# First column of the scan's addend made on ScalarE: three quarters of the scans begin from zero instead of from the carried state

## The chip, the cores and the metric

The program runs on one core of a Trainium2 chip. The core has five engines that each work through a queue of their own, in order: TensorE (PE, matmuls, with its weight loads shown apart as PEld), VectorE (DVE), ScalarE (ACT), GpSimd (POOL) and SyncE (SP, which here only issues transfers). They meet through semaphores. The metric is the device time of one execution in microseconds (us).

## The reference

Two layers follow each other, each as `x = x + layer(groupnorm(x))`, on an input of 4 x 512 x 64 x 64 in fp32. The second is a linear attention over 4096 positions. The first is what matters here: a layer norm over 512 channels, the channels cut into four chunks of 128, and for each chunk a Mamba block with 256 inner channels and 16 states per channel. Its heart is a recurrence over the 4096 positions of an image:

```python
dt = jax.nn.softplus(jnp.einsum('blr,er->ble', dt, dt_proj_w) + dt_proj_b)
A = -jnp.exp(A_log)

def step(h, inp):
    dt_t, B_t, C_t, x_t = inp
    dA = jnp.exp(dt_t[:, :, None] * A)
    h = dA * h + (dt_t * x_t)[:, :, None] * B_t[:, None, :]
    y = jnp.einsum('bds,bs->bd', h, C_t)
    return (h, y)
```

So for each of 4 images x 4 chunks x 256 channels x 16 states there is one scan `h[t] = dA[t] * h[t-1] + bx[t]` along 4096 positions, and the result is multiplied by C and summed over the 16 states.

## The kernel before

**Tiles.** The positions of an image are cut into 8 tiles of T = 512. A step is one triple (image b, tile t, chunk c), with c innermost: 4 x 8 x 4 = 128 steps, in `steps`. Within a step the 256 channels x 16 states are laid out as 32 groups of 128 partitions (32 channels x 4 states each), so a step has 32 scans of 128x512, and the program has 4096. Two scans make a slot; a step has SLOTS = 16 slots, numbered 0 to 15. Scan number k belongs to slot k // 2 of the whole program; `place` turns that number into the step n, the channel half e, the state group q and the half jj of the pair of slots.

**One scan.** Its operands come from three engines. `decay(k)` (L825) lets ACT write dA = exp(A * dt) into one of LEAD = 3 PSUM banks. `drive(g)` (L833) lets POOL make bx for both scans of slot g in one 128x1024 product, into one of 3 buffers. `slot` issues the scans on DVE (L851), with `tensor_tensor_scan`, whose initial value is the literal 0.0 in the first tile of an image (t == 0) and else a column of `st`, an SBUF tensor of 128x1 columns that holds the last value of the same scan one tile earlier. After every second slot POOL copies the four new last values into `st` (L862) and multiplies the last quarter of h by C (L863); DVE multiplies the first three quarters by C (L871, `product`), and PE folds the states (`fold_states`).

**Order.** The whole main loop is written out by hand in issue order, so each engine's queue is fixed when the program is built. In slot g: POOL's `drive(g + 2)`; then, for each of the two scans, the scan k on DVE and after it the exp of scan k + LEAD on ACT, which may start when scan k has given back its PSUM bank. Between the two scans (after the second in slot 10) of every even slot comes `product` of the slots before. After the two scans `after()` issues the step's other work by slot number: in slot 3 a softplus between two table loads on ACT (`time_steps`, L728, with table loads L1343 and L1345), in slot 10 the silu between two table loads (L1220, L1221, L1365), and in other slots copies of y, of projections, group and layer norms and the pieces of attention, many of which are ACT instructions. AWAY = (3, 10) names the two slots with the table loads.

**What one slot waits for.** A scan needs its dA (ACT), its bx (POOL) and, when it is the first of four, that PE is done with the h buffer. An exp needs a free PSUM bank, so the scan three before it. A drive needs the bx buffer of the slot three before it.

Of the kernel before, what the change touches and what calls it, by code (L numbers as in the profile page):

```python
# [10 lines left out]
AF = mybir.ActivationFunctionType  # L11
ALU = mybir.AluOpType
# [12 lines left out]
def kernel(  # L25
# [24 lines left out]
    nc = tc.nc  # L50
# [16 lines left out]
    LEAD = 3  # L67
# [338 lines left out]
    def bc(v, n):  # L406
        return v.unsqueeze(1).to_broadcast([P, n, v.shape[-1]])
# [346 lines left out]
    def mixers(f, nm):  # L754

        pd = work_bank(f"pd_{nm}", 0)
        for e in range(NH):
            mm(pd, w_xp[:, e, :], f["xz"][:, 0, e, :], start=(e == 0), stop=(e == NH - 1))  # L760
        yield
        f["both"] = wk.tile([P, 2, NH, T], F32, tag="dt", name=f"dt_{nm}", bufs=1)
        dtr = f["dtr"] = f["both"][0 : 2 * LANE, 1, NH - 1, :]
        nc.scalar.copy(dtr, pd[0 : 2 * LANE, :])
        b_rows = f["b_rows"] = dram.tile([NST, T], F32, tag="b_rows", name=f"b_rows_{nm}", bufs=3)
        c_rows = f["c_rows"] = dram.tile(
            [NST, T - CUT], F32, tag="c_rows", name=f"c_rows_{nm}", bufs=3
        )

        def rows_out():  # L770
            nc.sync.dma_start(b_rows, dtr[RANK : RANK + NST, :])
            nc.sync.dma_start(c_rows, dtr[LANE : LANE + NST, CUT:])

        later(1, rows_out)
        parts = f["parts"] = wk.tile([P, CUT], BF16, tag="parts", name=f"parts_{nm}", bufs=3)
        nc.scalar.copy(parts, pd[:, :CUT])
        for i in (2, 3):
            yield
            mm(pd[:, :CUT], minus, parts, start=False, stop=True, skip_group_check=True)
            yield  # L780
            nc.scalar.copy(parts[i * LANE :, :], pd[i * LANE :, :CUT])  # L781
# [4 lines left out]
    SLOTS = NH * NQ * JJ  # L786
    AWAY = (3, 10)

    def place(g):

        n, r = divmod(g, SLOTS)
        e, r = divmod(r, NQ * JJ)
        return n, e, *divmod(r, JJ)

    b_all, c_all, c_sb, dAs, bxs, hs, ys = {}, {}, {}, {}, {}, {}, {}
# [8 lines left out]
    def b_row(g):  # L804
        n, e, q, _ = place(g)
        b_all[g // JJ] = wk.tile([P, T], F32, tag="b_all", name=f"b_all_{g}", bufs=3)
        for_states(b_all[g // JJ], fs[n]["b_rows"], q)

    def c_tail(g):
        n, e, q, _ = place(g)  # L810
        c_sb[g // JJ] = wk.tile([P, T - CUT], F32, tag="c_sb", name=f"c_sb_{g}", bufs=2)
        for_states(c_sb[g // JJ], fs[n]["c_rows"], q)
# [7 lines left out]
    def decay(k):  # L820

        n, e, q, jj = place(k // 2)
        j = jj * 2 + k % 2
        dAs[k] = ps_d.tile([P, T], F32, tag="dA", name=f"dA_{k}")
        nc.scalar.activation(  # L825
            dAs[k], fs[n]["d_all", e][:, 0, j, :], AF.Exp, scale=a_t[:, e, j, q : q + 1]
        )

    def drive(g):

        n, e, q, jj = place(g)
        bxs[g] = wk.tile([P, 2, T], F32, tag="bx", name=f"bx_{g}", bufs=3)
        nc.gpsimd.tensor_tensor(  # L833
            bxs[g], fs[n]["d_all", e][:, 1, jj * 2 : jj * 2 + 2, :], bc(b_all[g // JJ], 2), ALU.mult
        )

    def slot(g, last, after):
        n, e, q, jj = place(g)
        b, t, c = steps[n]
        if g + 2 < last:  # L840
            drive(g + 2)
        if jj == 0:
            if g + 3 * JJ < last:
                b_row(g + 3 * JJ)
            hs[g // JJ] = wk.tile([P, NJ, T], F32, tag="h", name=f"h_{g}", bufs=2)
        elif g + 1 < last:
            c_tail(g + 1)
        h = hs[g // JJ]
        for i in range(2):
            j = jj * 2 + i  # L850
            nc.vector.tensor_tensor_scan(  # L851
                h[:, j, :], dAs.pop(2 * g + i), bxs[g][:, i, :],
                0.0 if t == 0 else st[:, c, e, q, j : j + 1], ALU.mult, ALU.add,
            )
            if 2 * g + i + LEAD < 2 * last:
                decay(2 * g + i + LEAD)
            if i == int(g % SLOTS == AWAY[1]) and jj == 0 and g:
                product(g - 1)
                fold_states(g - 1, last)
        del bxs[g]  # L860
        if jj == JJ - 1:
            nc.gpsimd.tensor_copy(st[:, c, e, q, :], h[:, :, T - 1])  # L862
            nc.gpsimd.tensor_tensor(  # L863
                h[:, :, CUT:], h[:, :, CUT:], bc(c_sb.pop(g // JJ), NJ), ALU.mult
            )
        after()

    def product(g):

        own = hs[g // JJ][:, :, :CUT]  # L870
        nc.vector.tensor_tensor(own, own, bc(c_all.pop(g // JJ), NJ), ALU.mult)  # L871

    def fold_states(g, last):

        n, e, q, _ = place(g)
        h = hs.pop(g // JJ)
        for j in range(NJ):
            mm(
                ys[n, e][j * BLK : (j + 1) * BLK, :], fold, h[:, j, :],
                start=False, stop=(q == NQ - 1), abreast=NJ,  # L880
            )
        if g + 1 < last:
            c_row(g + 1)
# [288 lines left out]
    steps = [(b, t, c) for b in range(B) for t in range(NT) for c in range(NC)]  # L1172
# [5 lines left out]
    st = const.tile([P, NC, NH, NQ, NJ], F32, tag="st", name="st")  # L1178
# [97 lines left out]
    first = mixers(fs[0], names[0])  # L1276
# [24 lines left out]
    for g in range(2):  # L1301
        drive(g)
# [6 lines left out]
    with tc.manual_schedule():  # L1309
        credit, seen, mix, held[0], held_x[0] = 0.0, work["mm"], iter(()), 0, 0  # L1310
        for n, (b, t, c) in enumerate(steps):
# [10 lines left out]
            for s in range(SLOTS):  # L1322
                def after():
# [69 lines left out]
                    seen = work["mm"]  # L1393

                slot(n * SLOTS + s, N * SLOTS, after)
            fs[n - 1].clear() if n else None
        product(N * SLOTS - 1)
# [64 lines left out]
```

## Time and profile before

| what | value |
|---|---|
| median of 3 runs | 7667.04 us (7658.92 to 7670.27) |
| the profiled execution's own time | 7665.56 us |
| its span | 7663.9 us |
| PE busy | 6445.6 us (84%) |
| DVE busy | 6950.2 us (91%) |
| ACT busy | 5455.4 us (71%) |
| POOL busy | 6890.5 us (90%) |

The profile is one execution. The first scan starts 95 us and the last 7237 us after the start of the span; what follows is attention on the last image, without scans. A group of the profile stands for all instructions of one line, engine, operation and shape, with its busy time, the mean of one in ns, and the idle time of the engine just before them with what ended it. A timeline row gives the start in us, the length of a run of equal instructions, and in square brackets the idle time before it. A row of the windows view gives the busy time of each engine between two moments.

### The profile page before, as it was taken

What the parts mean: (1) busy time and instruction counts of PE and PEld (TensorE: products, weight loads), DVE (VectorE), ACT (ScalarE), POOL (GpSimd) and SP (SyncE); (2) the same over time, 40 slices, a digit from 0 to 9 for tenths busy, and PEclk for the clock granted to TensorE, in tenths of its full rate; (3) what the DMA queues carried; (4) which work ended last, traced back from release to release, by engine and by line L of the source; (5) the groups of instructions that cost most, each with busy time, mean ns of one, the idle gap of its engine ahead of it and who ended that gap; (6) DMA issues with size and microseconds to landing.
All of it is one profiled execution on the core that took longest, in us unless ns stands there. A gap on an engine that the chain in (4) does not pass through costs nothing.

```text
span 7663.9 us, 93895 instructions
## 1 busy us (share of the span) xinstructions
PE 6445.6 (84%) x25507; PEld 2129.9 (28%) x25528; DVE 6950.2 (91%) x5720; ACT 5455.4 (71%) x8384; POOL 6890.5 (90%) x4638
## 2 busy tenths in 40 slices
PE   5677777777798899998788889898789999899799
PEld 2122222121232233332222233332223333233244
DVE  6999999999999999899999999999999999999821
ACT  5677777777777777777777777777777777777521
POOL 5999999999999999999999999999999999999700
PEclk8787877787899999999799999999889999999899
DMA  6666666666666666676666666667676666677502
GB/s 173 170 172 165 160 152 162 161 162 167 178 168 167 168 172 167 170 195 181 172 178 171 177 168 170 162 177 209 164 169 166 163 160 162 172 189 192 146 34 93
DMA packets 829233, 1265.55 MB, mean 165 GB/s; under 512 B 184072, under 2 KB 317720, under 8 KB 816416
## 3 DMA queue, kind: packets, MB, share of 16 engines
q1 hardware_dynamic: 806352, 1225.99, 61.6%
q0 software_dynamic: 16368, 32.51, 2.5%
q8 instruction: 204, 3.34, 0.2%
q14 instruction: 325, 2.66, 0.1%
q10 hardware_dynamic: 5984, 1.06, 0.1%
HBM read 1052.25 MB, written 206.57 MB: 164 GB/s over the span
## 4 chain that ended last, share of the span: by engine, by line
PE 28%; DVE 23%; DMA 13%; ACT 12%; issue 9%; POOL 9%; SPq 5%; POOLq 0%; DVEq 0%; ACTq 0%
DVE h L851 14%; DVE h L871 7%; PE pc L129 7%; POOL bx L833 6%; ACT dA L825 5%; DMA d_all<-d_rows 5%; DMA c_sb<-c_rows 4%; PE pq L129 4%; PE y L129 4%; SPq L800 4%; PE pp L129 3%; PE pr L129 3%; PE po L129 2%; DMA b_all<-b_rows 2%; DVE xn L440 2%
## 5 line engine op out<-in xcount | busy, mean ns | idle before, releaser
L833 POOL TENSOR_TENSOR bx<-d_all,b_all 128x1024 f32<-128x1024 f32 x2048 | 4825.1, 2369 | 105.5 <-DVE h L851 85.9
L851 DVE TENSOR_TENSOR_SCAN h<-dA,st,bx 128x512 f32<-128x512 f32 x3584 | 4351.8, 1267 | 252.7 <-PE y L129 99.0
L825 ACT ACTIVATE dA<-d_all,a_t 128x512 f32<-128x512 f32 x4096 | 2752.5, 687 | 1274.0 <-DVE h L851 1194.4
L129 PE MATMUL y<-h,fold 128*32 128x512 f32 x8192 | 1267.8, 685 | 850.7 <-DVE h L871 472.0
L871 DVE TENSOR_TENSOR h<-h,c_all 128x1536 f32<-128x1536 f32 x1024 | 1771.0, 1730 | 0.1
L863 POOL TENSOR_TENSOR h<-h,c_sb 128x512 f32<-128x512 f32 x1024 | 1301.2, 1271 | 116.8 <-DMA c_sb<-c_rows 32.3
L129 PE MATMUL pc<-xn,w_cv 128*128 128x512 f32 x2048 | 1109.1, 673 | 151.6 <-DVE xn L440 100.8
L129 PE MATMUL pq<-w_qk,xa 128*128 128x512 f32 x2048 | 958.1, 602 | 4.4 <-ACT xa L398 2.5
L129 PEld LDWEIGHTS y<-h,fold 128*32 128x32 f32 x8192 | 186.2, 113 | 1702.2 <-POOL h L863 880.5
L851 DVE TENSOR_TENSOR_SCAN h<-dA,bx 128x512 f32<-128x512 f32 x512 | 591.4, 1206 | 36.1 <-POOL bx L833 20.6
L129 PEld LDWEIGHTS pc<-xn,w_cv 128*128 128x128 f32 x2048 | 412.5, 210 | 712.1 <-issue 430.7
L129 PEld LDWEIGHTS pq<-w_qk,xa 128*128 128x128 f32 x2048 | 391.5, 194 | 461.3 <-issue 438.6
L129 PE MATMUL pr<-xb,m 128*128 128x512 f32 x1024 | 479.4, 607 | 4.1 <-ACT res L1142 2.2
L129 PE MATMUL pp<-xn,w_pr 128*128 128x512 f32 x1024 | 477.4, 593 | 4.7 <-ACT xr L563 4.7
L129 PEld LDWEIGHTS <-sel 128*128 128x128 bf16 x1216 | 116.6, 97 | 1064.0 <-issue 1062.3
L129 PE MATMUL c_all<-parts,sel 128*128 128x384 bf16 x1024 | 374.4, 366 | 0.6 <-ACT parts L781 0.6
L129 PE MATMUL y<-xz,dg 32*32 32x512 f32 x2048 | 317.1, 691 | 32.5 <-ACT xz L891 32.0
L894 POOL TENSOR_TENSOR xz<-xz 128x512 f32<-128x512 f32 x256 | 326.6, 1276 | 4.6 <-ACT xz L891 4.6
L736 POOL TENSOR_TENSOR dt<-dt,xz 128x1024 f32<-128x1024 f32 x127 | 300.1, 2363 | 0.6 <-ACT dt L728 0.6
L129 PE MATMUL pd<-xz,w_xp 128*128 128x512 f32 x512 | 295.3, 708 | 0.0
L129 PE MATMUL pz<-xn,w_z 128*128 128x512 f32 x512 | 261.6, 598 | 7.4 <-ACT kq L965 2.4
L129 PEld LDWEIGHTS pr<-xb,m 128*128 128x128 f32 x1024 | 195.8, 195 | 251.4 <-issue 220.0
(226 smaller groups left out, 6044.3 us busy)
## 6 DMA issues: line engine op xcount, KB each, us to landing
d_all<-d_rows SPq DMA_DIRECT2D x2040, 256.0 KB, 4.4
b_all<-b_rows SPq DMA_DIRECT2D x4096, 64.0 KB, 2.5
d_rows<-dt SPq DMA_DIRECT2D x254, 512.0 KB, 3.0
c_sb<-c_rows SPq DMA_DIRECT2D x4096, 16.0 KB, 3.5
xn<-in_x_dram SPq DMA_DIRECT2D x32, 1024.0 KB, 8.5
x<-xr SPq DMA_DIRECT2D x32, 1024.0 KB, 4.8
xa<-x SPq DMA_DIRECT2D x32, 1024.0 KB, 5.3
xb<-x SPq DMA_DIRECT2D x32, 1024.0 KB, 5.3
```

What stands on the lines that cost most here:

```text
L129: nc.tensor.matmul(out_, lhsT, rhs, **how)
L440: nc.vector.tensor_tensor(v, v, bc(m, NC), op)
L736: nc.gpsimd.tensor_tensor(f["both"][:, 1], f["both"][:, 0], f["xz"][:, 0], ALU.mult)
L800: nc.sync.dma_start(dst[k * BLK : (k + 1) * BLK, :], rows_[q * KS + k, :].partition_broadcast(BLK))
L825: nc.scalar.activation(dAs[k], fs[n]["d_all", e][:, 0, j, :], AF.Exp, scale=a_t[:, e, j, q : q + 1])
L833: nc.gpsimd.tensor_tensor(bxs[g], fs[n]["d_all", e][:, 1, jj * 2 : jj * 2 + 2, :], bc(b_all[g // JJ], 2), ALU.mult)
L851: nc.vector.tensor_tensor_scan(h[:, j, :], dAs.pop(2 * g + i), bxs[g][:, i, :], 0.0 if t == 0 else st[:, c, e, q, j : j + 1], ALU.mult, AL ...
L863: nc.gpsimd.tensor_tensor(h[:, :, CUT:], h[:, :, CUT:], bc(c_sb.pop(g // JJ), NJ), ALU.mult)
L871: nc.vector.tensor_tensor(own, own, bc(c_all.pop(g // JJ), NJ), ALU.mult)
L894: nc.gpsimd.tensor_tensor(f["xz"][:, 1, e, :], f["xz"][:, 1, e, :], f["xz"][:, 0, e, :], ALU.mult)
```

## The change

For a scan k that is not in the first tile of an image, and whose exp is issued in a slot other than 3, 4, 10 and 11 of its step (`carried`), the carried state is no longer the scan's initial value. Instead ACT, right behind the exp of that scan, rewrites the first column of its bx: bx[0] = dA[0] * st + bx[0], one activation (Identity) of 128x1 with two 128x1 operands, st as the scale and bx[0] as the bias (`carry`). The scan then begins from the literal 0.0. Of the 28 x 4 = 112 steps with t > 0, 12 of 16 slots are of that kind, which is 112 x 24 = 2688 scans; 896 scans keep the column of `st`, and 512 had 0.0 already.

```diff
+    def carried(k):
+
+        n, e, q, jj = place(k // 2)
+        return steps[n][1] and (k - LEAD) // 2 % SLOTS not in (3, 4, 10, 11)
+
+    def carry(k):
+
+        n, e, q, jj = place(k // 2)
+        c, j = steps[n][2], jj * 2 + k % 2
+        first = bxs[k // 2][:, k % 2, 0:1]
+        nc.scalar.activation(
+            first, dAs[k][:, 0:1], AF.Identity, bias=first, scale=st[:, c, e, q, j : j + 1]
+        )
+
@@ in slot
             nc.vector.tensor_tensor_scan(
                 h[:, j, :], dAs.pop(2 * g + i), bxs[g][:, i, :],
-                0.0 if t == 0 else st[:, c, e, q, j : j + 1], ALU.mult, ALU.add,
+                0.0 if t == 0 or carried(2 * g + i) else st[:, c, e, q, j : j + 1], ALU.mult, ALU.add,
             )
             if 2 * g + i + LEAD < 2 * last:
                 decay(2 * g + i + LEAD)
+                if carried(2 * g + i + LEAD):
+                    carry(2 * g + i + LEAD)
```

The queues of PE, DVE, POOL and SP keep their instructions and their order; ACT's gets 2688 instructions more. A carry waits for the exp before it and, where it is the first to touch a bx buffer, for the POOL instruction that fills that buffer. A scan waits for the carry where it waited for the exp. In the changed file the lines lie 14 or 16 further down: the exp stays L825, the carry is L839, drive is L847, the scan L865.

## The prediction

> **What bounds the kernel now.** I read the page first: busy shares, then the costliest groups.
>
> ```profile
> PE 6445.6 (84%) x25507; PEld 2129.9 (28%) x25528; DVE 6950.2 (91%) x5720; ACT 5455.4 (71%) x8384; POOL 6890.5 (90%) x4638
> ```
> ```profile
> L833 POOL TENSOR_TENSOR bx<-d_all,b_all 128x1024 f32<-128x1024 f32 x2048 | 4825.1, 2369 | 105.5 <-DVE h L851 85.9
> L851 DVE TENSOR_TENSOR_SCAN h<-dA,st,bx 128x512 f32<-128x512 f32 x3584 | 4351.8, 1267 | 252.7 <-PE y L129 99.0
> L825 ACT ACTIVATE dA<-d_all,a_t 128x512 f32<-128x512 f32 x4096 | 2752.5, 687 | 1274.0 <-DVE h L851 1194.4
> ...
> L851 DVE TENSOR_TENSOR_SCAN h<-dA,bx 128x512 f32<-128x512 f32 x512 | 591.4, 1206 | 36.1 <-POOL bx L833 20.6
> ```
>
> DVE and POOL are both near full. ACT's idle time is mostly waiting for a scan to give back a PSUM bank. Next the waits of DVE alone:
>
> ```profile
> DVE h L851 <- PE y L129: 109.0, 104, 3.1
> DVE h L851 <- ACT dA L825: 82.8, 131, 3.1
> DVE h L851 <- POOL bx L833: 72.8, 84, 4.2
> ```
>
> Then the windows view, cut at the first scan of each step: the four steps of image 0, tile 5, and the first two of image 1, tile 4. Columns: the stretch and its length, then busy us (and instructions) of PE, PEld, DVE, ACT, POOL, then the granted clock and DMA.
>
> ```profile
> 972.23:1027.66 55.43, 40.69 (x150) 10.52 (x150) 53.70 (x43) 40.30 (x60) 54.78 (x37) 0.78 0.66 162
> 1027.66:1080.76 53.10, 42.49 (x152) 10.87 (x152) 53.10 (x42) 42.24 (x63) 52.27 (x37) 0.74 0.59 150
> 1080.76:1137.55 56.79, 47.35 (x162) 14.54 (x162) 53.40 (x43) 38.43 (x56) 54.47 (x37) 0.85 0.59 141
> 1137.55:1190.73 53.18, 33.39 (x130) 9.00 (x130) 51.23 (x41) 40.10 (x66) 52.54 (x36) 0.81 0.77 188
> 2743.59:2798.36 54.77, 49.02 (x235) 16.36 (x234) 53.33 (x43) 45.40 (x70) 53.23 (x37) 1.00 0.64 164
> 2798.36:2853.49 55.13, 49.51 (x235) 17.03 (x234) 53.37 (x42) 44.55 (x69) 53.82 (x37) 1.00 0.65 163
> ```
>
> POOL is idle 0.65, 0.83, 2.32, 0.64, 1.54 and 1.31 us in these, DVE 1.73, 0, 3.39, 1.95, 1.44 and 1.76, ACT 9.4 to 18.4. So DVE and POOL bound the loop together, and about 0.6 us of POOL's idle per step looks like a floor. ACT has room on average; the question is where in the step.
>
> **What is removed.** DVE reads no column in 2688 scans. The price is the pitch of four scans in a row, once in an image's first tile and once later:
>
> ```profile
> 253.67 4.56 DVE L851 TENSOR_TENSOR_SCAN h<-dA,bx 128x512 f32<-128x512 f32 x4
> ```
> ```profile
> 3017.65 4.80 DVE L851 TENSOR_TENSOR_SCAN h<-dA,st,bx 128x512 f32<-128x512 f32 x4
> ```
>
> (4.80 - 4.56) / 4 = 0.06 us, as the means 1267 and 1206 say; 2688 x 0.06 = 161 us of DVE, 24 x 0.06 = 1.44 us per step. The end gets only what POOL can follow. Above its floor POOL gives 0.05, 0.23, 1.44, 0.04 us in the first four steps, mean 0.44; 0.94 and 0.71 in the others. With 0.44 for the 28 steps of image 0 and about 1.1 for the other 84 (the next two steps of image 1 have 2.8 and 2.1 us idle in the same view, so 1.44 each), it is 28 x 0.44 + 84 x 1.1 = 105 us. POOL's waits for DVE (bx 85.9, the st copy 28.8) give 115. Both are ceilings: a scan that is 0.06 shorter helps only where POOL stands waiting for that very scan. I take half, **-55 us**, and keep 0 and -105 as ends.
>
> **What is added: 2688 instructions on ACT.** No row shows this instruction. The nearest small one is
>
> ```profile
> L657 ACT ACTIVATE moff<-mv_first x4: 188/190/200, 497.6 to 5878.5; 128x4 f32<-128x4 f32 x4
> ```
>
> 0.19 us with constants. The carry has two 128x1 operands, as the Identity of L488 has (0.806 us for 512 columns). ACT copies of 256 and 512 columns take 0.366 and 0.584 (L965, L715), so 511 columns fewer take off 511 x 0.00085 = 0.43, which leaves 0.37. It reads what the exp wrote, so it starts after the exp's end: a pair like that stands at 58.80 (0.69 long) and 59.51, a gap of 0.02 to 0.03. Price 0.40 (ends 0.22 and 0.45, the last if overlap with the next instruction is lost): 2688 x 0.40 = 1075 us, 9.6 per step. The two-operand row is nearer in kind, so 0.40. In the second step above ACT would then stand at 42.24 + 9.6 = 51.8 of 53.10.
>
> The Trainium skill ("ScalarE: Activation LUTs", section "What ACT_TABLE_LOAD costs") gives a fixed 186 ns per ACTIVATE, 93 more for each such operand and an overlap of 93 between neighbours, so an estimate of 0.28 a carry and 753 us in all; the pair at 58.80 shows no overlap where the second reads the first, so the rows go ahead. Its "Rules for kernel authors" send multiply and add to VectorE rather than ScalarE, which speaks against this change: by the rows it trades 0.06 on one engine for 0.40 on the other.
>
> **Where that lies on the path.** ACT works in order, and its exps lead the scans by three. The sharpest place is the silu of slot 10. In the second step:
>
> ```profile
> 1064.20 1.29 ACT L825 ACTIVATE dA<-d_all,a_t 128x512 f32<-128x512 f32 x2
> ...
> 1070.09 1.30 ACT L825 ACTIVATE dA<-d_all,a_t 128x512 f32<-128x512 f32 x2
> ```
> ```profile
> 1070.86 4.81 DVE L851 TENSOR_TENSOR_SCAN h<-dA,st,bx 128x512 f32<-128x512 f32 x4
> ```
>
> The exp behind the silu ends at 1070.78, its scan starts at 1070.86. From 1047.63 to 1070.09 ACT is busy 21.11 of 22.46 us, and 10 carries (slots 5 to 9) add 4.0: ACT is 2.7 late there and DVE stands still for 2.6. Other steps have more room: 10 x 0.40 less ACT's idle time and the scan's margin, in the start times of the ACT and DVE rows, comes to 28 us in 26 of the 112 steps. The same sum for the softplus of slot 3 gives 2 us.
>
> Elsewhere a carry costs DVE the part of 0.40 that the exp does not lie ahead of its scan: 148 carried scans, 43 us together, 24 of them at slot 9, where five scans follow each other without a product between.
>
> **The new wait.** The first carry of each bx buffer waits for POOL. In 118 carried scans the scan starts within 0.40 of bx's end; now the carry lies between: 28 us. Behind a waiting carry stand the next exps, the copies of y (L891) and of the projections (L698, L563), and PE's banks wait for those. In 660 cases bx ends later than the exp, by 635 us together, at times when ACT mostly waited for DVE anyway. A running sum through ACT's rows, in which only idle time takes lateness away, gives 100 us of DVE stalls without this wait and 240 with it. The terms so far make 28 + 2 + 43 + 28 = 101; what the blocked queue adds lies between 0 and 140. I take 30, nearer to nothing, since most of ACT's idle time (1194 of 1274 us at the exps) is waiting for DVE.
>
> PE, POOL and SP keep their queues; no transfer is moved or added, and I cost them at nothing, since only DVE's pace times them. If POOL falls behind, the cover of bx goes, and that is the case of the second rival.
>
> **Sum** against the profiled execution, 7665.56 (1.5 below the median of the runs): -55 + 101 + 30 = +76, **about 7742 us**, 1% slower.
>
> **The rivals.**
>
> 1. Faster: the carries fall into ACT's waits for DVE (1194 us, against 1075 added) and POOL follows DVE. With 0.22 a carry the stalls are 4 + 18 + 11 = 33 us; -105 + 33 gives 7594, with half the relief 7644, so about 7610. For it speaks ACT's idle time; against it that steps of chunk 1 in image 0 keep 0.8 us on POOL and none on DVE. It decides once the stalls stay below the relief, with the 55 below about half of the above 101.
> 2. The wait for bx is worse than that: ACT is blocked in POOL's queue, stalls 240, relief 55 or less: 7850 or more. For it speak the 635 us; against it that scans waited for bx only 84 times.
> 3. Nothing: relief and stalls cancel within 15 us, 7650 to 7681.
> 4. The column isn't what the 0.06 us pays for, and scans keep 1267 ns: no relief, 131 us of stalls, 7797. Against it: two groups differ in nothing else by their shapes.
>
> **How the numbers follow.** Chances: my forecast 0.40, rival 1 0.27, rival 2 0.17, rival 3 0.09, rival 4 0.07. A measurement of this kernel can tell about 0.2% (15 us) from no change. So faster 0.27, same 0.09, slower 0.40 + 0.17 + 0.07 = 0.64. The range goes from rival 1's 7600, which leaves out about a quarter of it, to 7880, which leaves out the upper third of rival 2. My own case alone has 7690 to 7800.
>
> **What would show it.** The scans with two operands number 3200 at about 1206 ns, DVE's busy time falls by about 160. The carry has 2688 instructions of 0.35 to 0.40, ACT's busy time goes to about 6450. DVE's waits for ACT rise from 83 us to over 150, with the first scan after the silu among them; waits of ACT for POOL, now 33 us, appear at the carry. The prediction is wrong if DVE's wait for ACT stays under 100 us, if the carry takes under 0.25, or if POOL's busy time per step changes with DVE's pace.

## The result and the profile after

The changed kernel takes 7735.18 us (median of 5 runs, 7720.16 to 7745.31), the one before 7667.04. The ratio is 1.0091, with a 95% interval of 1.0079 to 1.0103: 0.9% slower. The profiled execution took 7726.49 us, its span 7724.8, which is 60.9 us above the execution profiled before.

The busy shares on the page of the changed kernel:

```profile
PE 6420.1 (83%) x25507; PEld 2123.9 (27%) x25528; DVE 6816.4 (88%) x5720; ACT 6230.8 (81%) x11072; POOL 6885.3 (89%) x4638
```

DVE does 134 us less, ACT 775 us more, POOL within 6 us of the same. The groups of the scan, the exp and the carry on the same page (busy time, mean ns | idle time before):

```profile
L865 DVE TENSOR_TENSOR_SCAN h<-dA,bx 128x512 f32<-128x512 f32 x3200 | 3720.1, 1205 | 325.4 <-ACT bx L839 210.2
L825 ACT ACTIVATE dA<-d_all,a_t 128x512 f32<-128x512 f32 x4096 | 2777.0, 687 | 458.1 <-DVE h L865 407.2
...
L839 ACT ACTIVATE bx<-dA,bx,st 128x1 f32<-128x1 f32 x2688 | 945.0, 352 | 374.8 <-POOL bx L847 215.4
L865 DVE TENSOR_TENSOR_SCAN h<-dA,st,bx 128x512 f32<-128x512 f32 x896 | 1100.4, 1265 | 160.8 <-ACT dA L825 96.8
```

The carried scans take 1205 ns, as those of an image's first tile did. The carry takes 0.352 us. ACT waited 1194 us for scans at its exps; now it waits 407, and 215 us more for POOL at the carry. The waits of DVE in the changed kernel:

```profile
DVE h L865 <- ACT bx L839: 213.5, 304, 2.3
...
DVE h L865 <- ACT dA L825: 111.5, 103, 3.1
DVE h L865 <- PE y L129: 84.0, 86, 3.2
...
DVE h L865 <- POOL bx L847: 20.5, 22, 1.8
```

Where DVE waited 83 us for ACT's exps, it waits 325 for exps and carries together. Its waits for POOL and PE fell from 73 and 109 to 21 and 84: at some of those scans POOL or PE came last before, and now ACT does. The windows of the same steps as before (the four steps of image 0, tile 5, and chunk 3 of image 1, tile 4, whose row of before stands last):

```profile
972.82:1028.18 55.36, 40.42 (x150) 10.05 (x150) 52.21 (x42) 46.56 (x84) 54.28 (x37) 0.75 0.64 162
1028.18:1082.63 54.45, 40.36 (x152) 10.66 (x152) 52.07 (x42) 49.97 (x89) 53.27 (x37) 0.81 0.57 147
1082.63:1137.69 55.06, 44.61 (x163) 14.18 (x162) 52.08 (x42) 45.17 (x81) 53.19 (x37) 0.91 0.57 144
1137.69:1191.53 53.84, 33.83 (x130) 8.75 (x130) 50.09 (x41) 46.69 (x91) 53.20 (x36) 0.81 0.78 187
...
2929.73:2988.32 58.59, 49.70 (x244) 17.98 (x246) 50.09 (x41) 50.68 (x100) 53.93 (x36) 0.97 0.71 175
```
```profile
2909.74:2966.28 56.54, 50.90 (x247) 18.32 (x248) 51.44 (x42) 43.10 (x74) 54.44 (x36) 0.97 0.77 190
```

The steps were 55.43, 53.10, 56.79 and 53.18 us, and the last one 56.54. Chunk 2, where POOL had 2.3 us to spare, gained 1.7; chunk 1, where POOL had 0.8 and DVE nothing, lost 1.35. Summed over all steps, from first scan to first scan (the last step to the end of its last scan), chunk 0 is 10 us longer, chunk 1 17 longer, chunk 2 23 shorter and chunk 3 56 longer, 60 in all; 52 of chunk 3's 56 are in images 1 to 3. The means of the steps with t > 0 in the trace before go the same way: a step of chunk 2 has ACT busy for 39.8 us and POOL idle for 2.9, one of chunk 3 for 41.9 and 1.4, of chunk 0 for 42.9 and 2.3, of chunk 1 for 44.3 and 2.1. So the steps with most room on both engines gain, and those where POOL has least to spare lose most. That is a match of means and no proof.

The silu begins with a table load. First that of the chunk 1 step before, then ACT around it in the timeline of the changed kernel, and DVE there:

```profile
1065.52 1.28 ACT L1220 ACT_TABLE_LOAD   x1
```
```profile
1065.06 0.35 ACT L839 ACTIVATE bx<-dA,bx,st 128x1 f32<-128x1 f32 x1
1065.31 0.57 ACT L715 COPY xz<-pz 128x512 f32<-128x512 f32 x1
...
1067.72 1.28 ACT L1236 ACT_TABLE_LOAD   x1
```
```profile
1060.76 2.34 DVE L865 TENSOR_TENSOR_SCAN h<-dA,bx 128x512 f32<-128x512 f32 x2 [0.56 <-ACT bx L839]
1064.42 1.22 DVE L865 TENSOR_TENSOR_SCAN h<-dA,bx 128x512 f32<-128x512 f32 x1 [1.33 <-ACT bx L839]
...
1073.02 2.46 DVE L865 TENSOR_TENSOR_SCAN h<-dA,st,bx 128x512 f32<-128x512 f32 x2 [0.49 <-ACT dA L825]
```

The table load of the silu starts 39.5 us after the step's first scan, where it started 37.9 us after it. DVE stands still 2.4 us over the carries and the silu, but the larger part is ahead of the silu, at the scans of slots 9 and 10. In the chunk 3 step DVE's largest waits for ACT are these:

```profile
2949.93 1.28 DVE L865 TENSOR_TENSOR_SCAN h<-dA,st,bx 128x512 f32<-128x512 f32 x1 [2.42 <-ACT dA L825]
...
2969.05 1.22 DVE L865 TENSOR_TENSOR_SCAN h<-dA,bx 128x512 f32<-128x512 f32 x1 [1.63 <-ACT bx L839]
```

The first stands behind the softplus block, the second ahead of the silu; in this step DVE waits 5.2 us for ACT in all, in the same step before 1.7.

### The profile page after: what moved, and what is told of

Its sections match the earlier page's. It is cut to its first block, busy times and chain, and to the rows that moved or that the text cites. A ratio compares the mean times of both kernels' runs of the same rounds, so it can differ in the third digit from the quotient of the medians.

```text
span 7724.8 us, 97324 instructions
## 1 busy us (share of the span) xinstructions
PE 6420.1 (83%) x25507; PEld 2123.9 (27%) x25528; DVE 6816.4 (88%) x5720; ACT 6230.8 (81%) x11072; POOL 6885.3 (89%) x4638
## 5 line engine op out<-in xcount | busy, mean ns | idle before, releaser
L847 POOL TENSOR_TENSOR bx<-d_all,b_all 128x1024 f32<-128x1024 f32 x2048 | 4823.1, 2367 | 112.4 <-DVE h L865 92.9
L865 DVE TENSOR_TENSOR_SCAN h<-dA,bx 128x512 f32<-128x512 f32 x3200 | 3720.1, 1205 | 325.4 <-ACT bx L839 210.2
L825 ACT ACTIVATE dA<-d_all,a_t 128x512 f32<-128x512 f32 x4096 | 2777.0, 687 | 458.1 <-DVE h L865 407.2
L839 ACT ACTIVATE bx<-dA,bx,st 128x1 f32<-128x1 f32 x2688 | 945.0, 352 | 374.8 <-POOL bx L847 215.4
L865 DVE TENSOR_TENSOR_SCAN h<-dA,st,bx 128x512 f32<-128x512 f32 x896 | 1100.4, 1265 | 160.8 <-ACT dA L825 96.8
L129 PE MATMUL pc<-xn,w_cv 128*128 128x512 f32 x2048 | 1087.7, 662 | 167.5 <-DVE xn L440 108.2
L878 POOL COPY st<-h 128x4 f32<-128x4 f32 x1024 | 208.1, 203 | 100.9 <-DVE h L865 92.1
```

The source lines that it names most:

```text
L129: nc.tensor.matmul(out_, lhsT, rhs, **how)
L825: nc.scalar.activation(dAs[k], fs[n]["d_all", e][:, 0, j, :], AF.Exp, scale=a_t[:, e, j, q : q + 1])
L839: nc.scalar.activation(first, dAs[k][:, 0:1], AF.Identity, bias=first, scale=st[:, c, e, q, j : j + 1])
L847: nc.gpsimd.tensor_tensor(bxs[g], fs[n]["d_all", e][:, 1, jj * 2 : jj * 2 + 2, :], bc(b_all[g // JJ], 2), ALU.mult)
L865: nc.vector.tensor_tensor_scan(h[:, j, :], dAs.pop(2 * g + i), bxs[g][:, i, :], 0.0 if t == 0 or carried(2 * g + i) else st[:, c, e, q, j ...
```

## Experiments

Each run has the time of the kernel before from the same chip beside it, and the ratio to it is what is compared. The intervals of two ratios make a difference between them uncertain by some 12 to 18 us. All edits are to the changed kernel.

**The relief alone.**

```diff
                 decay(2 * g + i + LEAD)
-                if carried(2 * g + i + LEAD):
-                    carry(2 * g + i + LEAD)
```

> Left out: the 2688 carries; those scans begin from zero and nothing replaces the carried state, so the state is lost there and only the relief of DVE remains. My theory (DVE is relieved of 0.06 us a scan, POOL lets about half through): 55 us faster, 7612, with 105 us (7562) as the ceiling. If the column is not what the 0.06 us pays for: no change, 7667, and the zero scans keep 1267 ns. If the wait for bx is the whole loss of the change, this run is 55 to 105 faster as well; it sets the size of the relief for the other runs.

Measured: 7616.03 us, ratio 0.9934 (0.9917 to 0.9951), 51 us faster by the ratio and near the 55 of the theory. The 0.06 us a scan is real, about a third of the 161 us comes through, and the rival that the column costs nothing is out. DVE's waits in this run:

```profile
DVE h L865 <- POOL bx L847: 144.7, 141, 6.2
DVE h L865 <- PE y L129: 131.9, 150, 3.5
DVE h L865 <- ACT dA L825: 101.8, 149, 2.2
```

Against before, the waits for POOL's bx doubled: a faster DVE comes sooner to where POOL is late.

**The carry into a spare tile.**

```diff
-        first = bxs[k // 2][:, k % 2, 0:1]
+        spare = small.tile([P, 1], F32, tag="spare", name=f"spare_{k}")
         nc.scalar.activation(
-            first, dAs[k][:, 0:1], AF.Identity, bias=first, scale=st[:, c, e, q, j : j + 1]
+            spare, dAs[k][:, 0:1], AF.Identity, bias=eps, scale=st[:, c, e, q, j : j + 1]
         )
```

> The carry writes its value into a spare 128x1 tile instead of bx (bias is a constant column), and the scans begin from zero, so the carried state is lost in 2688 scans. ACT does the same 2688 instructions behind the same exps, but none waits for POOL, and a scan waits for its exp alone. My theory (ACT's time is the larger part of the loss, 73 of 131 us): the relief plus about 73 for the late exps, some 20 us slower than before, 7685 (7650 to 7710). The rival (the wait for bx is the loss): the relief stays nearly whole, 7600 to 7625. The whole change has 7735.

Measured: 7680.79 us, ratio 1.0011 (0.9999 to 1.0023), which is 59 us above the relief alone by the ratios, and the whole change is another 61 above this. The time is the expected one, but a premise of the expectation was wrong: the scan did not wait for its exp alone. None of the 2688 carried scans began before the end of its carry, although it reads nothing of it, and 230 began 0.03 to 0.06 us behind it; the profile names the carry as what released such scans:

```profile
DVE h L865 <- ACT spare L839: 114.1, 174, 2.7
DVE h L865 <- PE y L129: 95.6, 104, 3.1
DVE h L865 <- POOL bx L847: 84.3, 92, 2.7
DVE h L865 <- ACT dA L825: 79.4, 88, 2.6
```

So this run holds ACT's time and the longer way from exp to scan. Of the 114 us for which scans waited for a carry, at most 55 lie between the end of the exp and the end of the carry (from the start times of the rows); the rest is a queue that was late already. What the run lacks of the whole change is the carry's wait for POOL and the write into bx; the two together are 61 us.

**One half of the carries each.**

```diff
-        return steps[n][1] and (k - LEAD) // 2 % SLOTS not in (3, 4, 10, 11)
+        return steps[n][1] and (k - LEAD) // 2 % SLOTS not in (3, 4, 10, 11) and k % 2 == 1
```

(the other with `k % 2 == 0`).

> Only the second scan of a slot is carried (odd numbers): 1344 carries, none of which is the first to touch its bx buffer, so none waits for POOL. Nothing is left out. My theory: half the relief (about -27), less than half of ACT's cost since lateness grows faster than load (about +25): 7667, within 20 us of before. The rival (wait for bx): all of the loss is gone and half of the relief is left, 7635 to 7645.

> Only the first scan of a slot is carried (even numbers): 1344 carries, all of which wait for the POOL instruction that fills bx. Nothing is left out. My theory: half the relief (-27), about 25 for ACT's time and 45 to 58 for the wait on bx and the queue behind it: 7710 (7690 to 7725). The rival (the wait for bx is the whole loss): the whole loss of 120 us or more with half the relief, 7750 or more.

Measured: second scans alone 7670.29 us, ratio 1.0001 (0.9992 to 1.0011); first scans alone 7717.91, ratio 1.0062 (1.0046 to 1.0078). Both are within the forecasts. ACT's waits for POOL and DVE's waits for ACT in the two, first scans first:

```profile
ACT bx L839 <- POOL bx L847: 327.1, 407, 3.9
```
```profile
DVE h L865 <- ACT dA L825: 202.9, 232, 3.0
...
DVE h L865 <- ACT bx L839: 34.5, 58, 1.9
```
```profile
ACT bx L839 <- POOL bx L847: 43.5, 57, 1.7
```
```profile
DVE h L865 <- ACT bx L839: 78.8, 140, 2.0
DVE h L865 <- ACT dA L825: 78.0, 87, 2.2
```

The two runs have as many carries and scans from zero as each other, and 47 us between them, which goes with the first carry's wait for bx: 327 us against 44. The 44 show that the expectation was wrong in one point: without a first carry the second one is the first to touch the buffer, and it finds POOL late 57 times. In the second run relief and ACT's cost cancel. The rival that the wait for bx is the whole loss is out, since nothing of the relief is left there.

The waits also show where the wait for bx lands. In the run with first scans alone, DVE waited 34.5 us for carries, which is first scans behind a carry of their own. Its waits for exps are 202.9, against 101.8 in the run without carries, and 178 of them (93 there) come at second scans, which have no carry in this run: their exps stand in the queue behind the carry that waits. So the larger part of the added waiting comes through ACT's queue (the carries' own time in it included) and not at the carry's own scan.

**The same wait without the write.** As the spare-tile run, with bx's first column as the bias.

```diff
-            first, dAs[k][:, 0:1], AF.Identity, bias=first, scale=st[:, c, e, q, j : j + 1]
+            spare, dAs[k][:, 0:1], AF.Identity, bias=first, scale=st[:, c, e, q, j : j + 1]
```

> As the run with the spare tile, but the carry takes bx's first column as its bias, so it waits for POOL as the real one does; it still writes the spare tile, and the scan waits for its exp alone (carried state lost in 2688 scans). The whole change is 54 us above the run with the spare tile. If that is the queue behind the waiting carry (my 30, bounds 0 and 140), this run lies 30 or more above it, 7710 or higher. If it is that the scan itself must wait 0.35 us longer, for the carry (my 28 + 43 by rows), it stays at 7681 to 7695.

Measured: 7741.92 us, ratio 1.0093 (1.0075 to 1.0111), the whole change again. The expectation rested on the same wrong premise: here too no waiting scan started before its carry's end. So the time of this run does not part the queue behind the carry from the later scan. It shows that putting the wait for bx back, without the write into bx, brings the 61 us back.

**The first carry behind the second exp.**

```diff
-                if carried(2 * g + i + LEAD):
-                    carry(2 * g + i + LEAD)
+                for m in (2 * g + i + LEAD - 1, 2 * g + i + LEAD) if (i + LEAD) % 2 else ():
+                    if carried(m):
+                        carry(m)
```

> The whole change, but the carry of a slot's first scan is issued behind the exp of the second one, with the second carry right after it. Nothing is left out. POOL has about 1.2 us more to fill bx before ACT asks for it. If the queue behind the wait is what costs 54 us, most of it goes: 7690 or less. If the longer way to the scan is what costs, the first scan of a slot is now later by up to a whole exp, and the run is at 7735 or above.

Measured: 7870.43 us, ratio 1.0259 (1.0240 to 1.0278), on the side of the longer way to the scan. Most of the wait for POOL went and a dearer one came:

```profile
ACT bx L839 <- POOL bx L847: 34.4, 41, 3.1
```
```profile
DVE h L865 <- ACT bx L839: 504.6, 531, 3.8
...
DVE h L865 <- ACT dA L825: 43.7, 58, 2.4
```

The second exp waits for the bank of the scan two before the carried one, so the one scan between, 1.21 us long, has to cover an exp of 0.69 and a carry of 0.35 with the gaps between. The lead of three scans had become a lead of two for half of the scans.

**ACT's time by itself.** A small instruction that touches neither dA nor bx, twice behind each exp in one run, and once, without the loop, in the other.

```diff
-        first = bxs[k // 2][:, k % 2, 0:1]
-        nc.scalar.activation(
-            first, dAs[k][:, 0:1], AF.Identity, bias=first, scale=st[:, c, e, q, j : j + 1]
-        )
+        old = st[:, c, e, q, j : j + 1]
+        for i in range(2):
+            spare = small.tile([P, 1], F32, tag=f"spare{i}", name=f"spare_{k}_{i}")
+            nc.scalar.activation(spare, old, AF.Identity, bias=eps, scale=old)
```

> In the runs with a spare tile every carried scan that had to wait for ACT began 0.03 us after the carry's end, not after the exp's, so those runs hold both ACT's time and the longer way to the scan. Here the small instruction reads st alone and writes a spare tile: it touches neither dA nor bx, so scan and POOL have nothing to do with it; the scans begin from zero (carried state lost in 2688 scans). It follows the exp without waiting for its end, so it takes ACT less, by the overlap of neighbours in the trace before about 0.28 instead of 0.40 us. If ACT's time is what the 65 us of the spare-tile run above the run without carries are: 65 x 0.28 / 0.40 = 45 above that run, 7660. If it is the longer way to the scan: at most 10 above it, 7626 or less. If both: 7626 to 7650.

> As the run with the detached small instruction, but with two of them behind each of the 2688 exps: ACT loses about 0.56 us an exp instead of 0.28, more than the 0.40 of the real carry, and still neither scan nor POOL has to do with it (carried state lost in 2688 scans). One of them cost 6 us above the run without carries (7622 against 7616). If ACT's time turns into late exps once the silu and softplus blocks slip, as my sum over the rows of before has it (28 and 2 us at 0.40, 8 at 0.28, 94 and 43 at 0.56), this run is some 137 us above the run without carries, 7753 (7710 or more). If ACT's time is free and only the longer way to the scan costs: 7640 or less, and then the 28 us of my sum were never there.

Measured: once 7621.65 us, ratio 0.9941 (0.9924 to 0.9958), some 5 us above the relief alone; twice 7824.65, ratio 1.0210 (1.0193 to 1.0227), 212 above it. In the timelines, from the start of an exp that is not held up to the start of the next instruction it is mostly 0.61 us in the kernel before, 0.89 with one such instruction between and 1.17 with two, so they take 0.28 and 0.56; with the real carry it is mostly 0.96 to 1.03, so 0.35 to 0.42. DVE's waits for exps, with one and with two:

```profile
DVE h L864 <- ACT dA L825: 127.2, 171, 3.2
```
```profile
DVE h L865 <- ACT dA L825: 286.1, 313, 2.9
```

By the first expectation, 7622 speaks for the longer way to the scan alone. The second run speaks against that: at 7825 it lies above even the 7753 for ACT's time. The first 750 us of ACT's time cost next to nothing, the second 750 cost 207, where the sum over the rows had 137 for the two together. ACT's room is used up in between, and the real carry's 0.35 to 0.42 lies there. So of the 59 us of the spare-tile run these runs leave open how much is lateness of the queue and how much the 0.38 us longer way from exp to scan (the carry and the gap before it); both exist, by the two-fold run and by the run with the later first carry.

**Carries only where there is room.**

```diff
-        return steps[n][1] and (k - LEAD) // 2 % SLOTS not in (3, 4, 10, 11)
+        s, c = (k - LEAD) // 2 % SLOTS, steps[n][2]
+        return steps[n][1] and s not in (3, 4, 10, 11) and (
+            c == 2 or k % 2 and s in (13, 14, 15, 0, 1)
+        )
```

(the run for chunk 2 alone has only `c == 2` there).

> Only steps of chunk 2 are carried (672 carries, 28 steps); nothing is left out. In the profiles the steps of chunk 2 are 23 us shorter in all with the whole change than before, those of the chunks 0, 1 and 3 are 10, 17 and 56 longer. If a step keeps its own gain and loss: 7645. If what one step gains is lost to POOL in the next: 7667.

> All 24 scans in steps of chunk 2, and elsewhere only second scans whose exps are issued in slots 13, 14, 15, 0 and 1, where ACT has most idle time and the carry never waits for POOL (672 + 420 carries; nothing is left out). If ACT's place in the step decides: 23 us from chunk 2 and half of 420 x 0.06 = 13 from the rest, 7630. If any carry costs more than it brings outside chunk 2: 7650 to 7665.

Measured: chunk 2 alone 7660.25 us, ratio 0.9983 (0.9972 to 0.9993), 13 us faster and between the two expectations: about half of what its steps gained in the whole change stays. With the second scans of slots 13 to 1 as well: 7640.20 us, ratio 0.9964 (0.9952 to 0.9976), again between the two expectations (7630, and 7650 or more), 28 us faster than before and faster than the changed kernel by about 1.3%. DVE's waits in that run, where the sum for ACT (131 us) stays nearer to the 83 of before than to the 325 of the whole change:

```profile
DVE h L868 <- ACT dA L825: 76.0, 110, 2.3
...
DVE h L868 <- ACT bx L842: 55.4, 87, 2.3
```

A fourth buffer for bx, 4 KB per partition, with the drives issued one slot earlier, might take the wait for POOL away; it wasn't tried.

## Why the prediction was right, point by point

The forecast was 7742 us, and it came out at 7735. The direction and the mechanism held: DVE's relief is real but only a part of it reaches the end, and late ACT work costs more than that. Two of the sizes were choices between bounds and not sums of rows, though: the half of the relief's ceiling, and the 30 between 0 and 140 for the blocked queue. That both fit is in part luck.

| term of the sum | forecast | measured, by ratios to before |
|---|---|---|
| relief, as far as POOL follows | -55 | -51 |
| late exps (28 + 2) and exps with too little lead (43) | +73 | +59 (spare tile above relief alone) |
| scan right behind bx (28) and queue behind the carry (30) | +58 | +61 (whole change above spare tile) |
| sum | +76 | +70 (whole change) |

- **Relief.** The half taken from a ceiling of 105 to 115 was the right size, with no row that gave the half. DVE's busy time fell by 134, not 160: the busy time joins scans that overlap, and scans that wait overlap less.
- **The carry's price.** 0.352 us long against the 0.37 worked out from the two-operand rows, and 0.35 to 0.42 of ACT's queue against 0.40. ACT's busy time rose by 775 us, to 6231 and not to 6450. The 6450 counts 2688 x 0.37 in full; the carries' own time is 945, and the instruction behind a carry can start before the carry's end (1065.31, where the carry runs to 1065.41), which busy time counts once. The Trainium skill's figures in "ScalarE: Activation LUTs", section "What ACT_TABLE_LOAD costs", are borne out by the detached instruction: 0.28 us of queue a piece with the overlap, and 0.375 long. The real carry doesn't have the overlap on its near side: it starts no sooner than 0.03 us after the end of its exp.
- **Where ACT is late.** The step shown for it, chunk 1 of image 0, was forecast to stand still 2.6 us behind the silu. It does so for 2.4, but only 0.5 behind the silu; lateness reaches the scans of slots 9 and 10 first, ahead of it. The largest loss, 52 us in the chunk 3 steps of images 1 to 3, was not named. In the one shown, DVE's waits for ACT went from 1.7 to 5.2 us, 2.4 of them at the softplus, which the sum had put at 2 us for the whole run.
- **Stalls and time.** The running sum gave 100 us of DVE stalls without the wait for bx and 240 with it. DVE's waits for ACT are 101.8 us in the run without carries, 193.5 with the spare tile and 325.0 with the whole change, so they rise by 92 and 223. The sum had the waits about right; the time rises by 59 and 120 only, and DVE's waits for POOL and PE fall meanwhile from 277 to 180 and 105, which fits scans that come late for ACT and then find the other two ready.
- **The wait for bx.** The sum of its two terms was right; in time they were not parted, since direct delay and blocked queue come and go together in every run. DVE's waits in the run with first scans alone put the direct delay there at 34.5 us at most and the rest on the queue, where the sum had 28 and 30. That scans waited for bx only 84 times, the argument against rival 2, said little: ACT asks for bx up to three scans sooner than DVE did, and waited 282 times.
- **Signs.** Of the signs that were named, DVE's waits for ACT (325 us, over 150), the scans' 1205 ns and the carry's length came as said. DVE's and ACT's busy time moved less than said, by 134 and 775. POOL's didn't follow DVE's pace: over the four steps of image 0, tile 5, it is 214.06 us before and 213.94 after.
- **Rivals.** Rival 1 needed the stalls below the relief; they cost 120 against 51. Rival 2's waits did come (242 us more of DVE waiting for ACT than before, against its 240), but they cost half of that in time, so its 7850 did not come. The relief run puts rival 4 out, and rival 3's range ends at 7681.

## What to carry to other kernels

An engine with idle time is not an engine with room: ask in which order its idle time lies and whose data a new instruction asks for, and how early. Here 2688 small instructions on ACT that ask for nothing, 0.28 us each, cost 5 us, while as many that read a fresh exp and a buffer filled just in time, and take 0.35 to 0.42 us for it, cost 120. Where an addition helps in some places of a loop and hurts in others, the step lengths by kind, before and after, show where to keep it: 1092 of the 2688 carries turned 0.9% slower into 0.4% faster.

## What was not expected of the hardware

ACT's cost is far from proportional: 0.28 us behind each of 2688 exps cost 5 us, 0.56 cost 212. And a scan can be held by an instruction whose result it doesn't need. In the run with the detached small instruction, 159 carried scans began within 0.06 us of the end of their exp, each while the small instruction behind the exp was still running. In the spare-tile run the carry reads one column of dA, as the scan does, and no scan began before the carry's end. One case of each, the detached instruction first (ACT, then DVE):

```profile
834.58 0.69 ACT L825 ACTIVATE dA<-d_all,a_t 128x512 f32<-128x512 f32 x1
835.19 0.39 ACT L840 ACTIVATE spare<-st,eps 128x1 f32<-128x1 f32 x1
```
```profile
835.30 1.22 DVE L864 TENSOR_TENSOR_SCAN h<-dA,bx 128x512 f32<-128x512 f32 x1 [0.67 <-ACT dA L825]
```
```profile
400.94 0.70 ACT L825 ACTIVATE dA<-d_all,a_t 128x512 f32<-128x512 f32 x1
401.67 0.35 ACT L839 ACTIVATE spare<-dA,eps,st 128x1 f32<-128x1 f32 x1
```
```profile
402.06 1.22 DVE L865 TENSOR_TENSOR_SCAN h<-dA,bx 128x512 f32<-128x512 f32 x1 [1.27 <-ACT spare L839]
```

In the trace, exp and carry raise the same semaphore, at 401.65 and 402.03, and the scan at 402.06 waits for that one alone. It let the first raise pass and began 0.02 us after the second. That points to an order that the program asks for and not to a stall of the chip; the count that the scan asked for isn't in the trace, so it is not shown.
